# Tiles' rows in a pool of their own and loaded before the down weights, the last routing at pair 20, layernorms in other places, x of five sequences on chip

## The chip, the cores and the metric

The kernel runs on one core of one Trainium2 chip. The metric is the device time of one execution in microseconds (us); less is better. The core has five engines that work in parallel, each through its own list of instructions in order: TensorE (PE: matrix products, and transposes through an identity; its weight loads are listed apart as PEld), VectorE (DVE), ScalarE (ACT), GpSimd (POOL) and SyncE (SP). They wait for each other through semaphores. Data move between the device's memory and the on-chip SBUF by DMA; here SP issues nearly all plain loads and stores, ACT a few at the start, and POOL those whose rows are chosen by an index (scatters and gathers, "indirect"). PE writes its results to PSUM, from which DVE and ACT take them.

## The reference

Four sublayers, each with a layernorm ahead and its input added behind, on x of 8 sequences x 512 tokens x 256 features in float32:

```python
x = x + _L0_attn_ref(_layernorm(x), Wq, Wk, Wv, Wo)                  # 16 heads of 16, 4 key heads, rotary, causal
x = x + _L0_ffn_ref(_layernorm(x), router_w, w_gate, w_up, w_down)   # 32 experts of 96, each token takes 8
x = x + _L1_attn_ref(_layernorm(x), w_qkv, b_qkv, w_out, b_out)      # 16 heads of 16, causal
x = x + _L1_ffn_ref(_layernorm(x), gate_w, w1, w2, w3, sw1, sw2, sw3)# 16 experts of 176, each token takes 2, one shared of 352

def _layernorm(x, axis=-1, eps=1e-05):
    m = jnp.mean(x, axis=axis, keepdims=True)
    v = jnp.var(x, axis=axis, keepdims=True)
    return (x - m) / jnp.sqrt(v + eps)

# attention: softmax(q k^T / 4, causal) v, then the product with the out weights
# an expert layer: probs = softmax(x @ router); the k largest are a token's experts; weights rw
for e in experts:                       # layer 0: rw divided by their sum
    w_e = sum(where(sel == e, rw, 0), axis=-1)
    y += (silu(x @ wg[e]) * (x @ wu[e])) @ wd[e] * w_e[:, None]
```

## The kernel before, in words

**Stages.** The program goes through four stages: attention 0 for eight sequences (to about 609 us of the span), the experts of layer 0 (to about 1119), attention 1 (to about 1668), the experts of layer 1 (to about 1902), and a short end. `pipeline` interleaves in attention, while PE works on the scores of sequence b, the preparation of a later sequence (`before`: input, layernorm, projections) and the finish of the previous one (`finish`: `Attention.output`, then `after0` or `after1`, with layernorm, routing and in layer 1 the shared expert). The parts are Python generators; how far each is advanced at each step fixes the order of the program, and a scheduler then orders each engine's list. For PE in the expert stages the order is the written one (`manual_schedule`). `tc.issue_after(inst)` forbids that an instruction be placed ahead of `inst` in that order; it is no wait on the chip.

**Attention.** A sequence has four chunks of four heads (`NCK`). `scores` makes the products of keys and queries (L680) and their exponentials on ACT (L685), `mask` multiplies the diagonal blocks by a causal mask on DVE (L691), `values` makes the product with v (L703), copies it out (L709), transposes it (L716), and divides by the row sums on DVE: a reciprocal `rec` (L719) and a product into `otok` (L720). `output` first updates `fine` (two DVE instructions, L754 and L755), transposes `otok` (L761), multiplies by the out weights (`y_a`, L769) and adds to x.

**Layernorm.** `layernorm_steps` takes the statistics of the four tiles of 128 tokens (L315, L316), then `inverse_root` finds 1/sqrt(v) with integer arithmetic and three Newton steps (L281 to L290, a dozen small DVE instructions, each needing the one ahead of it), then xn = (x - m) * rstd (L325). `turned` transposes it on PE (L343).

**Routing.** For each sequence, `routed0` (layer 0) or `after1` (layer 1) takes the layernorm, the router's product, and the k largest (`route`). Each token's normalized row, with its weights behind it, is written to the rows of its experts in a table `xg` in device memory: 4 x 8 = 32 scatters of 128 rows per sequence in layer 0 and 4 x 2 = 8 in layer 1 (L427). Each layer's sequences fall into two parts with tables of their own: 0 to 3 and 4 to 7 in layer 0, 0 to 5 and 6 to 7 in layer 1 (`SPLIT = (4, 6)`). When a part's last sequence is routed, `tables` works out which tiles of 128 rows belong to which expert, and stores zeros behind each expert's last row (SP, L1076). In layer 0 the routing of sequence 7 isn't in attention 0 but beside the first part's experts.

**Experts.** `experts` goes through pairs of tiles of 128 rows: 75 + 75 pairs in layer 0 and 30 + 14 in layer 1. Step s of its loop does, in this order: `load` of pair s (two SP loads of 144 KB, L1141, after reading eight row numbers into registers at every fourth pair), `turn_x` of pair s - 4 (transposes L1150, copy by DVE L1152), `gate_up` of pair s - 5 (L1183, silu on ACT, products on DVE L1175), `turn_h` of pair s - 6 (L1203, copy L1204) and `down` of pair s - 7 (`y_m`, L1214, copy by ACT L1219). Layer 0 stores the result in order (SP, L1221) and gathers it by token later (POOL, L1263); layer 1 scatters it to the tokens' rows (POOL, L1225), and `results` loads them in order. At s == 3 `load_last()` issues the load of the down weights `dw` (`load_down`, L1303: six transfers in layer 0, 26 in layer 1, some 3 MB either way). PE's `y_m` for any pair reads the whole tile `dw`, whose part is chosen by a register.

The pool of `xg` tiles (seven buffers) is the pool `mp` of the other tiles of the experts, `dw` has a pool `dwp`. Pools are stacked in SBUF, and those of one stage lie where the pools of the stage before lay: the first use of an address waits for its last use there.

**Beside the experts.** `beside.add(first, last, steps, work)` spreads the steps of a generator over the pairs from `first` to `last`. In layer 0: the store of x of sequence 7, its routing (pairs 7 to 20), the tables of the second part (22 to 54), the loads of attention 1's weights, the first loads of x for attention 1 with their gathers; in layer 1: `results` of sequences 0 to 5.

**x.** `xs[b]` lives in a ring of five buffers in SBUF. After attention 0 every sequence's x is stored to `x_after[0]` and fetched again. In layer 1, `after1` stores x of sequences 0 to 5 to `x_after[1]` (`keep_x`), and `results` loads them again (`x_c`, L1331), adds the experts' results (L1348), transposes and stores the output; sequences 6 and 7 are left in their buffers.

**Start.** `fast0` loads q, k, v, cos and sin weights. k and v share the one buffer `kv_in`, cos and sin the one buffer `turnf`; those four loads are issued by ACT (L847, L858). PE turns cos and sin through transposes (L861) before the input (L1321).

Of the kernel before, what the change touches and what calls it, by code (L numbers as in the profile page):

```python
# [22 lines left out]
NG = 4  # L23
NCK = H // NG
E0, K0, I0 = 32, 8, 96
E1, K1, I1, IS1 = 16, 2, 176, 352
# [65 lines left out]
def two_blocks_kernel(  # L92
# [63 lines left out]
    def new_x(b, name):  # L156
        xs[b] = xpool.tile([P, NT, D], F32, tag="x", name=f"x_{name}_{b}", bufs=5)
        return xs[b]
# [146 lines left out]
    def layernorm_steps(x, lnp, name, tag="xn", bufs=1, spare=0, behind=lambda: None):  # L305


        def later():
            return tc.issue_after(behind()) if behind() else ExitStack()
# [12 lines left out]
        xn = lnp.tile([P, NT, D + spare], F32, tag=tag, name=f"xn_{name}", bufs=bufs)  # L322
        for t in range(NT):
            with later():
                nc.vector.tensor_scalar(  # L325
                    xn[:, t, :D], x[:, t, :], mv[:, t, 0:1], rstd[:, t : t + 1], ALU.subtract, ALU.mult
                )
            if t % 2:
                yield
        return xn  # L330
# [326 lines left out]
    class Attention:  # L657
# [6 lines left out]
        def __init__(self, n, late, ptp, ps, bank, wo, masked=None):  # L664
            self.n, self.fine, self.late, self.ptp, self.ps, self.bank, self.wo = n, fines[n], late, ptp, ps, bank, wo
            self.heads, self.otok, self.rec = {}, {}, {}
            self.last = iter(())
            self.masked = masked

# [25 lines left out]
        def values(self, b, c, probs):  # L695
# [19 lines left out]
            for t in range(NT):  # L715
# [3 lines left out]
            nc.vector.reciprocal(rec, ot[:, :, :, ONE])  # L719
            nc.vector.tensor_tensor(  # L720
                self.otok[b][:, :, c, :, :], ot[:, :, :, :DH],
                rec.unsqueeze(3).to_broadcast([P, NT, NG, DH]), ALU.mult,
            )
            yield
# [107 lines left out]
    def fast0(awp, lnp, atp, late, ptp, ps, bank):  # L832
# [11 lines left out]
        for n, which in enumerate("kv"):  # L844
            lo, hi = A0[which]
            kv_in = awp.tile([P, ND, NG, 32], F32, tag="kv_in", name=f"{which}_in", bufs=1)
            nc.scalar.dma_start(out=kv_in.rearrange("p k g r -> p (k g r)"), in_=a0[:, lo:hi])  # L847
            at = D + n * HKV * DH
            nc.vector.tensor_copy(
                wq[:, :, at : at + HKV * DH].rearrange("p k (g d) -> p k g d", g=HKV), kv_in[:, :, :, :DH]  # L850
            )
# [3 lines left out]
        for which in ("cos", "sin"):  # L855
            lo, hi = A0[which]
            f = awp.tile([DH, T], F32, tag="turnf", name=f"{which}f", bufs=1)
            nc.scalar.dma_start(out=f, in_=a0[:DH, lo:hi])  # L858
# [13 lines left out]
        def before(b):  # L872
# [4 lines left out]
            x = xs[b]  # L877
            xn = layernorm(x, lnp, name)
            yield from free()
            xn = yield from turned(xn, lnp, bank, name)  # L880
# [84 lines left out]

    def fast1(w, v1s, lnp, atp, late, ptp, ps, bank, last):
        wv, wo, vb, ob, qkb = (w[n] for n in ("v", "o", "vb", "ob", "qkb"))
        att = Attention(1, late, ptp, ps, bank, wo, last)

        def before(b):  # L970
            x, name = xs[b], f"a1_{b}"
            xn = layernorm(x, lnp, name, behind=att.masked)
            yield from free()
# [107 lines left out]
    class Beside:  # L1081


        def __init__(self, *items):
            self.items = []
            for item in items:
                self.add(*item)
            self.load = None
            self.last = None

        def add(self, first, last, steps, work):
# [13 lines left out]

    def experts(n, gu, dn, mp, ps, again, beside, load_last):

# [27 lines left out]
        def load(lay, i):  # L1135
            part = lay.part
            if i % RB == 0:
                registers(lay, i)
            xg = mp.tile([P, 2, lay.width], F32, tag="xg", name=f"xg_{name}_{part}_{i}", bufs=7)
            for j in range(2):  # L1140
# [55 lines left out]
        def turn_h(lay, i):  # L1196
# [4 lines left out]
            for q, (lo, n_in) in enumerate(chunks):  # L1201
                for j in range(2):
                    nc.tensor.transpose(hp[:n_in, q, j, :], h[:, j, lo : lo + n_in], ident)  # L1203
            beside.last = nc.vector.tensor_copy(hT[: chunks[0][1]], hp[: chunks[0][1]]).ins  # L1204
            made["hT", part, i] = hT

# [81 lines left out]

    def load_down(w, src, inner, routed):

# [7 lines left out]
        for n, lo, hi, e, at in pieces(inner, whole):  # L1298
            while lo < hi:
                q, r = at // width, at % width  # L1300
                rows = min(hi - lo, width - r)
                to = (e * chunks + q) * D
                nc.sync.dma_start(out=w[r : r + rows, :, to : to + D], in_=src[n, lo : lo + rows, :, 2 * ND * P :])  # L1303
                lo, at = lo + rows, at + rows
# [20 lines left out]
    def results(seqs, gat, op, ps, again="", behind=lambda: None):  # L1325


        def begin(b):
            if b < SPLIT[1]:
                xs[b] = gat.tile([P, NT, D], F32, tag="x", name=f"x_c1{again}_{b}", bufs=3)  # L1330
# [68 lines left out]
    def all_experts(n, gw, gat, again=False, weights=()):  # L1399
# [6 lines left out]
        with ExitStack() as s:  # L1406
            dwp = s.enter_context(tc.tile_pool(name=f"down{n}{g}", bufs=1, reuse_waits="tile"))
            mp = s.enter_context(tc.tile_pool(name=f"moe{n}{g}", bufs=3, reuse_waits="tile"))
            small = s.enter_context(tc.tile_pool(name=f"tables{n}{g}", bufs=1, reuse_waits="tile"))
            ps = s.enter_context(tc.tile_pool(name=f"ps_m{n}{g}", bufs=2, space=PSUM, reuse_waits="tile"))  # L1410
# [29 lines left out]
            if n == 0 and not again:  # L1440
                beside.add(8, 9, 1, x_kept())
                lnp = s.enter_context(tc.tile_pool(name="ln_last", bufs=1, reuse_waits="tile"))
                beside.add(7, 20, 13, routed0(NB - 1, lnp, bank, ffn_parts(lnp, bank)[0], lambda: beside.last))
                begin = 22
            beside.add(
# [48 lines left out]
    with ExitStack() as s1:  # L1494
        wp1 = s1.enter_context(tc.tile_pool(name="attn_w1", bufs=1, reuse_waits="tile"))
        gat = s1.enter_context(tc.tile_pool(name="gather", bufs=1, reuse_waits="tile"))
        w1, loads1 = weights1(wp1)
        last = all_experts(0, gw0, gat, weights=loads1)
        with ExitStack() as s:
            awp, lnp, atp, late, ptp, smp, ps = pools(s, 1, False)  # L1500
            v1s = v_tiles(awp, 2, H, nc.vector)
            bank = banks(ps, 3)
            att, before = fast1(w1, v1s, lnp, atp, late, ptp, ps, bank, last)
            route, shared = ffn_parts(smp, bank)
# [12 lines left out]
            def after1(b):  # L1517
# [58 lines left out]
    def general1(gat):  # L1576
        with ExitStack() as s:
# [20 lines left out]
            def all_of(b, name):  # L1598
# [7 lines left out]
                yield from shared(sw1, xT, xs[b], name)  # L1606
                if b < SPLIT[1]:
                    keep_x(b, x_after[1])
# [178 lines left out]
```

## Time and profile before

| | us |
|---|---|
| median of 14 runs | 1936.32 (1933.41 to 1954.11) |
| the profiled execution's own time | 1929.41 |
| its span, first to last instruction | 1927.6 |
| PE busy | 1591.6 (83%) |
| DVE busy | 993.8 (52%) |
| ACT busy | 650.0 (34%) |
| POOL busy | 811.6 (42%) |
| L427 scatters on POOL | 316.0 in 320 instructions |
| L1263 gathers on POOL | 403.6 in 256 instructions |

The mean granted clock of PE is 0.901. All engine times come from the one profiled execution, which is 0.36% shorter than the median of the runs. The chain that ended last, followed back from the end, spends 64% of the span on PE, 11% on "another core or an unknown queue", 9% on DVE, 7% on issue, 4% on ACT and 2% on DMA.

How to read it: a row of a timeline or of the chain begins with the start and the length in us, then engine and line, the operation, and the tiles written and read (`out<-in`); `x8` counts the instructions that the row takes together, and its length runs from the first one's start to the last one's end. SPq and ACTq are the queues' issues of DMAs, not the transfers. A row of waits reads: who waited, for whom, us in total, times, longest. Line numbers are those of the kernel before; in the changed kernel the same statements stand up to 20 lines lower.

### The profile page before, as it was taken

Reading aid. Unit: us, or ns where it says so; the run is one execution under the profiler, and the core shown is the slowest. Engines: PE = TensorE matmul, PEld = TensorE weight load, DVE = VectorE, ACT = ScalarE, POOL = GpSimd, SP = SyncE. Lnnn points to the kernel's source line nnn. Section 1 sums busy time; section 2 is a strip of 40 time slices with the busy share of each in tenths; the row PEclk is TensorE's granted clock in tenths of the full one; section 3 lists DMA queues with packets and bytes.
Section 4 is the critical chain, followed back from the end, with each engine's and each line's share of the span. In section 5 each row is a group of like instructions: output and inputs, shape, how many; then the busy total and the mean of one; then the engine's idle time right before and its main releaser. Section 6 shows DMA issues by size and latency. Waiting matters only on the chain.

```text
span 1927.6 us, 31020 instructions
## 1 busy us (share of the span) xinstructions
PE 1591.6 (83%) x10180; PEld 1050.0 (54%) x10180; DVE 993.8 (52%) x3179; ACT 650.0 (34%) x865; POOL 811.6 (42%) x686
## 2 busy tenths in 40 slices
PE   5976394666755758999999979998999998999995
PEld 3433142333423747989998844445444544677764
DVE  5664272544623424545555666576556645444453
ACT  3533152233312212323333335454444443222222
POOL 0041614414254160000778888488885011243332
PEclk9987696878868778999999989999999998999997
DMA  2032322522124655787999974356643022435364
GB/s 65 28 104 78 109 80 90 167 102 72 64 95 142 203 171 168 216 252 203 255 257 275 282 139 69 70 99 130 132 75 68 21 85 74 142 99 160 93 217 154
DMA packets 245721, 255.75 MB, mean 133 GB/s; under 512 B 79881, under 2 KB 224911, under 8 KB 245554
## 3 DMA queue, kind: packets, MB, share of 16 engines
q1 hardware_dynamic: 188754, 164.15, 28.6%
q0 software_dynamic: 56448, 89.18, 20.2%
q8 instruction: 88, 1.44, 0.3%
q14 instruction: 79, 0.65, 0.1%
q10 hardware_dynamic: 352, 0.33, 0.1%
HBM read 132.37 MB, written 124.32 MB: 133 GB/s over the span
## 4 chain that ended last, share of the span: by engine, by line
PE 64%; another core or an unknown queue 11%; DVE 9%; issue 7%; ACT 4%; DMA 2%; SPq 1%; POOL 0%; DVEq 0%; POOLq 0%; ACTq 0%
PE gu_m L1183 13%; PE y_m L1214 8%; PE st_a L680 8%; PE o_a L703 6%; PE xgT_m L1150 4%; ACT p_a L685 3%; PE y_a L769 3%; PE hT_m L1203 2%; PE sy_f L457 2%; PE su_f L444 2%; PE qkv_a L887 2%; PE sg_f L444 2%; DVE p_a L691 2%; PE q_a L998 2%
## 5 line engine op out<-in xcount | busy, mean ns | idle before, releaser
L427 POOL DMA_INDIRECT xg<-xn_f,rows_f x320 | 316.0, 987 | 648.3 <-DVE rec_a L719 241.2
L1263 POOL DMA_INDIRECT x_a<-yg,yrows x256 | 403.6, 1577 | 292.7 <-DVE yrows L1260 194.0
L685 ACT ACTIVATE p_a<-st_a 128x2048 f32<-128x2048 f32 (+1 forms) x192 | 306.1, 1594 | 372.9 <-PE st_a L680 229.6
L1183 PE MATMUL gu_m<-gw,xgTs_m 128*128 x1552 | 339.9, 363 | 26.7 <-DVE xgTs_m L1152 25.5
L1183 PEld LDWEIGHTS gu_m<-gw,xgTs_m 128*128 128x128 f32 x1552 | 261.6, 194 | 56.9 <-DVE xgTs_m L1152 26.9
L680 PE MATMUL st_a<-qT_a,kT_a 32*128 32x512 f32 (+3 forms) x2048 | 219.3, 502 | 60.2 <-ACT p_a L685 38.6
L1214 PE MATMUL y_m<-dw,hTs_m 96*128 (+1 forms) x952 | 239.6, 382 | 0.0
L703 PE MATMUL o_a<-p_a,v 128*32 128x512 f32 (+3 forms) x2048 | 211.3, 471 | 26.8 <-issue 20.7
L691 DVE TENSOR_TENSOR p_a<-p_a,causal 128x512 f32<-128x512 f32 x256 | 170.7, 685 | 119.7 <-ACT p_a L685 111.4
L1152 DVE COPY xgTs_m<-xgT_m 128x512 f32<-128x512 f32 x194 | 133.6, 689 | 108.5 <-PE xgT_m L1150 66.6
L680 PEld LDWEIGHTS st_a<-qT_a,kT_a 32*128 32x128 f32 x2048 | 97.7, 198 | 163.1 <-issue 77.8
L1219 ACT COPY ys_m<-y_m 128x512 f32<-128x512 f32 x194 | 113.7, 586 | 207.8 <-PE y_m L1214 150.1
L1214 PEld LDWEIGHTS y_m<-dw,hTs_m 96*128 96x128 f32 (+1 forms) x952 | 166.5, 191 | 15.5
L1175 DVE SCALAR_TENSOR_TENSOR h_m<-h_m,xg_m,gu_m 128x96 f32<-128x96 f32 (+1 forms) x388 | 114.6, 326 | 90.3 <-ACT h_m L1188 37.0
L1225 POOL DMA_INDIRECT yg<-ys_m,to_m x88 | 88.9, 1010 | 152.8 <-ACT ys_m L1219 138.2
L1204 DVE COPY hTs_m<-hT_m 96x256 f32<-96x256 f32 (+1 forms) x194 | 92.8, 478 | 116.7 <-PE hT_m L1203 77.6
L1150 PE MATMUL xgT_m<-ident,xg_m 128*128 128x128 f32 x776 | 121.9, 279 | 19.2 <-DMA xg_m<-xg 9.1
L1191 ACT ACTIVATE h_m<-gu_m 128x192 f32<-128x192 f32 x150 | 49.7, 331 | 245.7 <-PE gu_m L1183 141.5
L703 PEld LDWEIGHTS o_a<-p_a,v 128*32 128x32 f32 x2048 | 51.9, 112 | 135.8 <-issue 95.3
L709 DVE COPY osb_a<-o_a 128x512 f32<-128x512 f32 x64 | 44.0, 688 | 158.4 <-remote 61.4
L1150 PEld LDWEIGHTS xgT_m<-ident,xg_m 128*128 128x128 f32 x776 | 97.2, 144 | 43.2 <-issue 20.5
L769 PE MATMUL y_a<-wo,oT_a 128*128 128x256 f32 x256 | 78.7, 452 | 30.9 <-issue 24.1
(206 smaller groups left out, 1712.0 us busy)
## 6 DMA issues: line engine op xcount, KB each, us to landing
xg_m<-xg SPq DMA_DIRECT2D x388, 144.0 KB
yg<-ys_m SPq DMA_DIRECT2D x150, 256.0 KB
xg<-zeros SPq DMA_DIRECT2D x100, 144.0 KB
g<-yg SPq DMA_DIRECT2D x16, 512.0 KB
xg<-xn_f,rows_f POOLq DMA_INDIRECT x320
x_after<-x_in SPq DMA_DIRECT2D x8, 512.0 KB
x_a<-x_after SPq DMA_DIRECT2D x8, 512.0 KB
x_a<-yg,yrows POOLq DMA_INDIRECT x256
```

Of the source, the lines that this page charges most:

```text
L427: inst = nc.gpsimd.indirect_dma_start(out=lay.xg, out_offset=bass.IndirectOffsetOnAxis(ap=rows[:, t, i : i + 1], axis=0), in_=xn[:, t, :], ...
L680: nc.tensor.matmul(st[:, g, at : at + T - j * P], kT[r, j * P : (j + 1) * P], qT[r, j * P :], start=True, stop=True,)
L685: nc.scalar.activation(pt, st[:, :, :width], AF.Exp, scale=SCALE)
L691: self.masked = nc.vector.tensor_tensor(d, d, causal.unsqueeze(1).to_broadcast([P, NG, P]), ALU.mult).ins
L703: nc.tensor.matmul(o[32 * g : 32 * g + 32, j * P :], v1[:, j, v_at + g * (DH + 1) :][:, :32], probs[n][:, g, at : at + T - j * P], start=( ...
L769: nc.tensor.matmul(y[:, i, :], oT[:, k, t * P : (t + 1) * P], self.wo[:, k, :], start=(k == 0), stop=(k == ND - 1),)
L1150: nc.tensor.transpose(tr[:, j, c, :], xg[:, j, c * P : (c + 1) * P], ident)
L1152: nc.vector.tensor_copy(xT, tr)
L1175: nc.vector.scalar_tensor_tensor(h[:, j, :], h[:, j, :], xg[:, j, D:][:, bass.ds(offs[part, i + j][2], 1)], gus[j][:, inner:], ALU.mult, A ...
L1183: nc.tensor.matmul(gus[j], xT[:, j, c, :], gu[:, bass.ds(at + c * 2 * inner, 2 * inner)], start=(c == 0), stop=(c == ND - 1),)
L1214: nc.tensor.matmul(y[:, j, :], hT[:n_in, q, j, :], dn[:n_in, bass.ds(at + q * D, D)], start=(q == 0), stop=(q == n_ch - 1),)
L1263: nc.gpsimd.indirect_dma_start(out=xs[b][:, t, :], out_offset=None, in_=lay.yg[: lay.tiles(bool(again)) * P, :], in_offset=bass.IndirectOf ...
```

## The change

- Tiles' rows: `xg` tiles get a pool of their own, `xgp` ("rows"), opened after `mp`, with seven buffers as before. `load_down` now issues each transfer of `dw` only after the last row load that had been issued by then (`beside.load`), that is, after the eight of pairs 0 to 3.
- Last routing: the routing of sequence 7 in layer 0 goes to pairs 20 to 33 instead of 7 to 20, and the second part's tables to pairs 36 to 68 instead of 22 to 54.
- Normalizations: in attention 0, the layernorm of the next sequence may not be placed ahead of the last product into `otok` made by then, and for sequences 2 and on it is written two steps later, with as many steps fewer behind it. In attention 1, the layernorm of sequence 0 is written instruction by instruction behind the last six `hT` copies of the experts of layer 0 (two of its instructions per copy) instead of all behind the last copy.
- x: sequences 3 to 7 stay in the ring of five (`XS`); only sequences 0 to 2 are stored in `after1` and loaded in `results`.
- Start: two buffers each for `kv_in` and `turnf`.

The program that redoes the work when the fast one's bounds don't hold, which isn't run on these inputs, is changed in the same way.

```diff
+XS = 5
...
     def new_x(b, name):
-        xs[b] = xpool.tile([P, NT, D], F32, tag="x", name=f"x_{name}_{b}", bufs=5)
+        xs[b] = xpool.tile([P, NT, D], F32, tag="x", name=f"x_{name}_{b}", bufs=XS)
...
+            self.normed = None
...
-            nc.vector.tensor_tensor(
+            self.normed = nc.vector.tensor_tensor(
                 self.otok[b][:, :, c, :, :], ot[:, :, :, :DH],
                 rec.unsqueeze(3).to_broadcast([P, NT, NG, DH]), ALU.mult,
-            )
+            ).ins
...
-            kv_in = awp.tile([P, ND, NG, 32], F32, tag="kv_in", name=f"{which}_in", bufs=1)
+            kv_in = awp.tile([P, ND, NG, 32], F32, tag="kv_in", name=f"{which}_in", bufs=2)
...
-            f = awp.tile([DH, T], F32, tag="turnf", name=f"{which}f", bufs=1)
+            f = awp.tile([DH, T], F32, tag="turnf", name=f"{which}f", bufs=2)
...
             x = xs[b]
-            xn = layernorm(x, lnp, name)
-            yield from free()
+            if b > 1:
+                yield
+                yield
+            xn = layernorm(x, lnp, name, behind=att.normed)
+            for _ in range(4 if b < 2 else 2):
+                yield
             xn = yield from turned(xn, lnp, bank, name)
...
-    def fast1(w, v1s, lnp, atp, late, ptp, ps, bank, last):
+    def fast1(w, v1s, lnp, atp, late, ptp, ps, bank, copies):
-        att = Attention(1, late, ptp, ps, bank, wo, last)
+        att = Attention(1, late, ptp, ps, bank, wo, copies[-1])
...
-            xn = layernorm(x, lnp, name, behind=att.masked)
+            if b == 0:
+                behind = iter([copy for copy in copies[-6:] for _ in range(2)])
+                xn = whole(layernorm_steps(x, lnp, name, behind=lambda: next(behind)))
+            else:
+                xn = layernorm(x, lnp, name, behind=att.masked)
...
-    def experts(n, gu, dn, mp, ps, again, beside, load_last):
+    def experts(n, gu, dn, mp, xgp, ps, again, beside, load_last):
...
-            xg = mp.tile([P, 2, lay.width], F32, tag="xg", name=f"xg_{name}_{part}_{i}", bufs=7)
+            xg = xgp.tile([P, 2, lay.width], F32, tag="xg", name=f"xg_{name}_{part}_{i}")
...
             beside.last = nc.vector.tensor_copy(hT[: chunks[0][1]], hp[: chunks[0][1]]).ins
+            beside.copies.append(beside.last)
...
-    def load_down(w, src, inner, routed):
+    def load_down(w, src, inner, routed, behind):
...
-                nc.sync.dma_start(out=w[r : r + rows, :, to : to + D], in_=src[n, lo : lo + rows, :, 2 * ND * P :])
+                with tc.issue_after(behind):
+                    nc.sync.dma_start(out=w[r : r + rows, :, to : to + D], in_=src[n, lo : lo + rows, :, 2 * ND * P :])
...
         def begin(b):
-            if b < SPLIT[1]:
+            if b < NB - XS:
                 xs[b] = gat.tile([P, NT, D], F32, tag="x", name=f"x_c1{again}_{b}", bufs=3)
...
             mp = s.enter_context(tc.tile_pool(name=f"moe{n}{g}", bufs=3, reuse_waits="tile"))
+            xgp = s.enter_context(tc.tile_pool(name=f"rows{n}{g}", bufs=7, reuse_waits="tile"))
...
-                beside.add(7, 20, 13, routed0(NB - 1, lnp, bank, ffn_parts(lnp, bank)[0], lambda: beside.last))
-                begin = 22
+                beside.add(20, 33, 13, routed0(NB - 1, lnp, bank, ffn_parts(lnp, bank)[0], lambda: beside.last))
+                begin = 36
...
-            experts(n, gw, dw, mp, ps, again, beside, lambda: load_down(dw, src, inner, routed))
-            return beside.last
+            experts(n, gw, dw, mp, xgp, ps, again, beside, lambda: load_down(dw, src, inner, routed, beside.load))
+            return beside.copies
...
-                if b < SPLIT[1]:
+                if b < NB - XS:
                     keep_x(b, x_after[1])
```

More of the change, by code (lines that the diff above doesn't have):

```diff
@@ L308, in later @@
         def later():
-            return tc.issue_after(behind()) if behind() else ExitStack()
+            inst = behind()
+            return tc.issue_after(inst) if inst else ExitStack()
         stats = lnp.tile([P, NT, 6], F32, tag="stats", name=f"stats_{name}")
@@ L1089, in __init__ @@
             self.last = None
+            self.copies = []
         def add(self, first, last, steps, work):
@@ L1497, in two_blocks_kernel @@
         w1, loads1 = weights1(wp1)
-        last = all_experts(0, gw0, gat, weights=loads1)
+        copies = all_experts(0, gw0, gat, weights=loads1)
         with ExitStack() as s:
@@ L1502, in two_blocks_kernel @@
             bank = banks(ps, 3)
-            att, before = fast1(w1, v1s, lnp, atp, late, ptp, ps, bank, last)
+            att, before = fast1(w1, v1s, lnp, atp, late, ptp, ps, bank, copies)
             route, shared = ffn_parts(smp, bank)
@@ L1606, in all_of @@
                 yield from shared(sw1, xT, xs[b], name)
-                if b < SPLIT[1]:
+                if b < NB - XS:
                     keep_x(b, x_after[1])
```

## The prediction

> **What bounds the kernel now.** I read the page's engine rows first: TensorE (PE) is busy 83% of the span, so a change can only pay where PE stands still or where it would stand still afterwards. Then a table of windows cut at the stages tells where that is. Its columns are length, then busy time and instruction count of PE, weight load, VectorE (DVE), ScalarE (ACT) and GpSimd (POOL), the granted clock, the DMA share and GB/s.
>
> ```profile
> 605.00:640.00 35.00, 9.85 (x36) 7.19 (x34) 2.36 (x4) 1.87 (x2) 23.55 (x25) 0.60 0.66 203
> 640.00:655.00 15.00, 14.54 (x76) 13.81 (x77) 9.67 (x31) 3.41 (x8) 0.00 (x0) 0.80 0.83 237
> ...
> 690.00:740.00 50.00, 18.64 (x83) 15.34 (x82) 7.86 (x21) 4.47 (x10) 26.51 (x28) 0.62 0.42 141
> 740.00:820.00 80.00, 79.54 (x506) 72.93 (x505) 45.61 (x125) 24.77 (x55) 0.00 (x0) 1.00 0.69 206
> ...
> 1590.00:1670.00 80.00, 70.16 (x384) 38.95 (x383) 40.28 (x165) 21.79 (x24) 15.73 (x16) 0.89 0.36 99
> 1670.00:1766.00 96.00, 96.00 (x465) 72.50 (x465) 46.66 (x144) 22.68 (x57) 33.53 (x34) 1.00 0.42 132
> ```
>
> Two things are to be seen. Both expert stages, once running, are PE without a gap (79.54 of 80, 96.00 of 96), so a late start of either is not made up later. And in 605–640 and 690–740 every compute engine is nearly idle while POOL issues the 32 scatters of one sequence's rows (L427). By the instructions' start times there are eight such bursts of about 41 us (the first from 116.0, the last 684.5 to 725.3), and in each the gaps over 1 us that PE, DVE and ACT have together sum to 13.5 to 26.3 us. I call that the standstill; its cause is not in the profile, and the bursts of 8 scatters in attention 1 show none.
>
> Then the waits of PE at the places the diff touches, the start of the chain that ended last, and SyncE (SP), which issues the loads:
>
> ```profile
> PE oT_a L761 <- DVE rstd_a L290: 1.8, 1, 1.8
> PE o_a L703 <- DVE p_a L691: 0.4, 1, 0.4
> ...
> PE xT_a L343 <- DVE xn_a L325: 3.3, 1, 3.3
> ```
> ```profile
> 1.25 2.42 DMA cosf<-in_a_dram
> ...
> 4.42 4.98 DMA sinf<-in_a_dram
> ```
> ```profile
> 600.99 2.57 SPq L1303 DMA_DIRECT2D dw<-in_f_dram  x4
> 604.63 34.32 SPq L1141 DMA_DIRECT2D xg_m<-xg  x8
> 638.96 1.40 SPq L1303 DMA_DIRECT2D dw<-in_f_dram  x2
> ...
> 1624.61 13.86 SPq L1303 DMA_DIRECT2D dw<-in_f_dram  x26
> 1639.60 9.27 SPq L1141 DMA_DIRECT2D xg_m<-xg  x14
> ```
> ```profile
> 646.74 1.03 PE L1214 MATMUL y_m<-dw,hTs_m 96*128 x4
> ...
> 1678.76 1.89 PE L1214 MATMUL y_m<-dw,hTs_m 88*128 x8
> 1680.48 0.60 PE L1150 MATMUL xgT_m<-ident,xg_m 128*128 128x128 f32 x4
> ```
>
> **The change, part by part,** against the profiled execution: 1929.41 us, span 1927.6 (1.8 around it), 6.9 us or 0.36% under the median 1936.32 of 14 runs. I take each difference over to the median unchanged.
>
> *Start of attention 0 (two buffers for kv_in and turnf).* The load of sinf is issued at 4.42, after cosf's buffer is free, and lands 4.98 later. PE takes its transposes first (9.45) and the input's behind them (9.99), though xf had landed by 6. With two buffers sinf and v_in are issued some 2.5 us earlier. Next in line on DVE is q_in's copy (landed 8.45, 0.62 us) and the bias (9.21), and the changed order puts stats_a ahead of five small instructions. I put stats_a's first instruction at 9.9 instead of 11.76, where the chain shows it: −2, between −0.5 (q_in is late too) and −3.5.
>
> *Layernorm behind the last normalization in attention 0.* At the one clean turn from a sequence to the next (75 to 90), stats and the 14-step rstd chain stand on DVE ahead of the reciprocal and product that oT needs: PE waits 1.8 + 0.4 us. The same DVE work now comes behind; its xn is needed only 60 us later, so it costs nothing there: −2.2. Six more turns lie in or at the edge of a burst, where the waits shown (8.8, 11.6 and 23.1 us) contain the standstill. Each is worth between 0, if the standstill covers it, and 2.2; I take 1: −6 (0 to −13).
>
> *Layernorm of attention 1's first sequence, woven behind the last hT copies.* The row of 3.3 us goes: 5.7 us of DVE work starts behind the last six pairs instead of after the last. A pair lasts 2.83 us and DVE is busy 45.61 of 80 in it, so some 1.2 us per pair are free: over five pairs it fits. It may delay hT copies by one 0.4 us instruction each. −3, between −4 and −1.
>
> *Rows ahead of down weights, experts 0.* Now the first xg load waits for the last y_a of attention (ends 608.8), and six dw loads (3.15 MB) go behind eight xg loads. Before, four of them (2.05 MB) went at 601 to 603.6 and landed during the standstill, at no cost. In it, SP gets on at 0.70 us per item, 4.2 us for a pair of loads; the second pair, which also waited for y_a, got through at 619.4 (SP's own rows), which I take for the first now, three more pairs reach 632 to 636, and dw is issued by about 639. At the 237 GB/s of the row for 640–655, 3.15 MB take 13.3 us: landed at 652 to 653 against a first y_m at 646.74. Nothing else of PE can pass y_m. +6, between +2 (the loads get through early) and +12 (the next pair's rows, queued behind dw, come after it).
>
> The Trainium skill (DMA: Bandwidth & Descriptors, "Anatomy of one DMA") fits a transfer, measured on GpSimd's path, at 2.0 us plus its bytes over 436 GB/s. By it dw would be there 9.2 us after its issue, an estimate from that page, at 648, and this term would be +1.5. The window row shows 237 GB/s with the engines 83% taken, so I stay with the row.
>
> *The same, experts 1.* Before, the 26 dw loads were out by 1638.5, 40 us ahead of the first y_m. Now the first xg load waits for the shared expert's su of sequence 6 (about 1642, harmless) and the second pair for all eight scatters of sequence 7, whose issues end at 1664.9; I take 1666.5 for their landing, about as long after as an issue and a half. Three pairs need 2.6 us, the 26 loads 13.9 as before, about 2 us to land the last (cosf's 32 KB took 2.42): some 1685 against 1678.76. The fifth pair's rows, behind dw, land near 1687 against 1680.48. Both give +6 to +7, and the second is covered by the first. +6, between +2 (2.88 MB at 237 GB/s need only 12.2 us from 1668.5) and +12 (scatters land later).
>
> *Last routing at pairs 20 to 33 instead of 7 to 20.* Its PE and DVE instructions and POOL's 32 scatters are the same; POOL has no other DMA between 725 and the gathers from 919, so its order stays. The burst meets the same kind of pairs, and what it stops is again PE-bound. The tables go from pairs 22–54 to 36–68, and with them 33 stores of zeros (144 KB each) on SP's queue, still ahead of the second part's first load at pair 75; the yg stores there go past single xg loads. 0, between −13 (a standstill of 13.5, the least seen, for 26.3) and +10 (the zeros meet the prefetch).
>
> *x of five sequences on chip.* Three stores of 512 KB in attention 1 and three loads in experts 1 (issued 1858, 1869, 1880) go, and results of sequences 3 to 5 take a step less each. DMA share there is 0.36 to 0.48, SP is not on the chain, and the end hangs on the last scatter, its load and two additions, all unchanged: 0, between −2 and 0.
>
> Sum: −2 − 2.2 − 6 − 3 + 6 + 6 = −1.2. Span 1926.4, execution 1928.2, median about **1935 us**.
>
> **The rivals.** 0.3% (5.8 us) is about what a measurement of this kernel can tell from no change: under 1930.5 is faster, over 1942.1 slower.
>
> Slower: dw behind the rows, at both stages. For it: PE cannot go round y_m, and the rates are the trace's. If the six turns in bursts give 0, the start −0.5, attention 1 −1, and both waits are +12: −2.2 − 1.5 + 24 = +20, 1956. It decides once the waits together exceed what the layernorms give by 6. Against it: SP may leave the standstill sooner.
>
> Faster: all seven turns give 2.2 (−15.4), start −3.5, attention 1 −4, both waits +2: −19, 1917. For it: the rows of waits are there at each turn, and DVE holds 9% of the chain. Against it: a standstill takes whatever lies in it.
>
> The standstill changes with its place: 13.5 instead of 26.3 takes 13 off, 1922; a collision adds 10, 1945. For it: the spread of the eight; against: the two bursts beside expert work were the long ones.
>
> That keeping x on chip changes nothing is in the sum already.
>
> **How the numbers follow.** The sum (own range 1928 to 1942) 0.35: 0.08 of that faster, 0.25 same, 0.02 slower. Late weights 0.31: 0.29 slower, 0.02 same. All turns paying 0.25, faster. Another standstill 0.09: 0.06 faster, 0.03 slower. So 0.39, 0.27, 0.34. The range 1916 to 1957 reaches both outer cases.
>
> **What would show it.** Stats of sequence 0 near 9.9; no wait of oT for rstd at 80; xT right behind the last y_m of experts 0; first y_m waiting for dw's DMA, 6 us later against the last y_a and against the end of attention 1; the standstill of the last burst near 26 us. The prediction fails if the bursts in attention 0 change length, since their sum of 170 us is far above every term here, or if dw gets out before the standstill ends.

## The result

| | us |
|---|---|
| before, median (47 runs) | 1936.57 (1931.63 to 1958.35) |
| changed, median (10 runs) | 1961.51 (1957.42 to 1974.45) |
| ratio, 95% interval | 1.0124 [1.0095, 1.0153] |
| changed, the profiled execution | 1947.03, span 1945.3 |

The changed kernel is 1.2% slower; the median lies 4.5 us above the predicted range. The two profiled executions differ by 17.6 us, the medians by 25: the profiled execution is 14.5 us under the median of the changed kernel, where that of before was 6.9 under its own.

The experiments further down ran on four chips on which all times are some 14% lower: the kernel before has a median of 1658 to 1660 us on each of them, and the changed kernel is 1.0019 [1.0003, 1.0036] of it. How the two settings differ is told with the experiments; first the two traces of the first setting, which the prediction was about.

The start of the same instruction in both traces shows where the time went (us of the span; the last column is what the stretch since the row above gained or lost):

| place | before | changed | difference | of it in this stretch |
|---|---|---|---|---|
| first stats of attention 0 | 11.76 | 9.59 | -2.2 | -2.2 |
| last y_a of sequence 0 (end) | 92.07 | 85.64 | -6.4 | -4.3 |
| last y_a of sequence 4 (end) | 416.46 | 406.21 | -10.3 | -3.8 |
| last y_a of sequence 7 (end) | 608.81 | 605.40 | -3.4 | +6.8 |
| first y_m of layer 0 | 646.74 | 648.80 | +2.1 | +5.5 |
| pair 15 | 682.07 | 682.94 | +0.9 | -1.2 |
| pair 35 (past both routings) | 777.62 | 780.54 | +2.9 | +2.1 |
| pair 75 | 896.78 | 904.44 | +7.7 | +4.7 |
| first xT_a of attention 1 | 1121.93 | 1126.64 | +4.7 | -3.0 |
| last y_a of attention 1 (end) | 1632.30 | 1638.41 | +6.1 | +1.4 |
| first y_m of layer 1 | 1678.76 | 1693.87 | +15.1 | +9.0 |
| pair 8 of layer 1 | 1700.97 | 1719.53 | +18.6 | +3.4 |
| end of PE | 1918.35 | 1937.10 | +18.8 | +0.2 |

The windows of the changed kernel, the same as of before and four more around the start of layer 1 (columns as there):

```profile
605.00:640.00 35.00, 9.93 (x33) 6.98 (x33) 3.79 (x9) 1.83 (x3) 21.23 (x23) 0.65 0.62 181
640.00:655.00 15.00, 9.74 (x40) 8.77 (x40) 3.69 (x10) 1.36 (x4) 0.00 (x0) 0.68 0.98 236
...
690.00:740.00 50.00, 44.78 (x288) 41.12 (x286) 28.12 (x107) 15.66 (x31) 10.90 (x12) 0.97 0.65 198
740.00:820.00 80.00, 54.52 (x312) 48.47 (x313) 29.59 (x86) 16.30 (x36) 19.88 (x21) 0.81 0.53 161
...
1670.00:1766.00 96.00, 89.04 (x405) 65.97 (x404) 42.62 (x133) 18.37 (x46) 26.35 (x28) 0.93 0.52 148
...
1674.00:1684.00 10.00, 6.83 (x22) 4.31 (x23) 3.86 (x19) 0.63 (x2) 0.00 (x0) 0.66 0.85 214
1684.00:1694.00 10.00, 6.45 (x32) 4.39 (x31) 4.42 (x10) 1.27 (x4) 0.00 (x0) 1.00 0.89 199
1694.00:1702.00 8.00, 8.00 (x22) 5.56 (x23) 2.80 (x14) 0.91 (x2) 2.00 (x2) 0.57 0.88 262
1702.00:1720.00 18.00, 18.00 (x94) 13.94 (x92) 8.41 (x24) 4.25 (x11) 5.91 (x6) 1.00 0.44 147
```

In 640 to 655 PE is busy 9.74 of 15 us where it had been 14.54, and the DMA engines are full (0.98, 236 GB/s): the down weights are on their way. In layer 1 the 96 us that had been without a gap hold 7 us of idle time, and in two short stretches the granted clock is 0.66 and 0.57 where it had been 1.00. Cut at the clock's own changes, these are two stretches of 6.8 us at half the clock, with full clock between them:

```profile
1677.13:1683.95 6.82, 5.41 (x11) 3.31 (x12) 2.42 (x9) 0.63 (x2) 0.00 (x0) 0.50 0.84 197
1683.95:1694.19 10.24, 6.69 (x33) 4.61 (x32) 4.55 (x10) 1.27 (x5) 0.00 (x0) 1.00 0.89 202
1694.19:1701.02 6.83, 6.83 (x18) 4.80 (x17) 2.41 (x13) 0.91 (x2) 2.00 (x2) 0.50 0.86 256
```

The standstill has moved from 690–740 to 740–820.

PE's and SP's timelines of the changed kernel at the two starts:

```profile
633.87 3.51 SPq L1319 DMA_DIRECT2D dw<-in_f_dram  x6
637.58 12.66 SPq L1155 DMA_DIRECT2D xg_m<-xg  x9
...
1648.85 26.20 SPq L1155 DMA_DIRECT2D xg_m<-xg  x8
1675.16 14.04 SPq L1319 DMA_DIRECT2D dw<-in_f_dram  x26
1690.32 7.25 SPq L1155 DMA_DIRECT2D xg_m<-xg  x12
```
```profile
648.80 2.04 PE L1229 MATMUL y_m<-dw,hTs_m 96*128 x4 [5.26 <-DMA xg_m<-xg]
...
1678.54 5.06 PE L1197 MATMUL gu_m<-gw,xgTs_m 128*128 x8 [2.69 <-DVE xgTs_m L1166]
...
1684.11 2.53 PE L1197 MATMUL gu_m<-gw,xgTs_m 128*128 x8
...
1693.87 3.44 PE L1229 MATMUL y_m<-dw,hTs_m 88*128 x8 [3.55 <-DMA xg_m<-xg]
1697.10 1.06 PE L1164 MATMUL xgT_m<-ident,xg_m 128*128 128x128 f32 x4
1697.95 4.05 PE L1197 MATMUL gu_m<-gw,xgTs_m 128*128 x8
```

The brackets put y_m's waits down to a row load, but it is dw that came late: among the semaphores that y_m waits for is that of the last dw load, and the trace has its last update at 648.71 in layer 0 and at 1693.73 in layer 1, where y_m begins at 648.80 and 1693.87. In layer 1 that load was issued at 1688.85, so it took 4.9 us to land.

Added up by PE's time, the 12.4 us of layer 1 (9.0 to the first y_m, 3.4 more to pair 8) have three parts. PE stands 2.69 us since DVE's list has small `to_m` instructions of later pairs ahead of the first copy of xT, and four of those wait for rows that come late (2.1 us together); it stands 3.55 for dw. The third part is the slower clock: the same eight gu_m matmuls take 5.06 and 4.05 us where they take 2.53 at full clock, and y_m 3.44 for 1.89; that is 5.6 us, nearly as much as both stops together. Along the path these parts don't all count. y_m begins when dw is there, whatever PE did before, so the first stop and the slow gu_m after it lie inside the wait for dw. The 9.0 us are the late dw, and the 3.4 behind them are the half clock after the second stop.

And the zeros of the second part's tables (SP's timeline, and PE's waits from 820 to 905), which now lie in pairs 55 to 68:

```profile
840.67 4.48 SPq L1089 DMA_DIRECT2D xg<-zeros  x9
...
863.28 3.99 SPq L1089 DMA_DIRECT2D xg<-zeros  x8
...
874.76 5.06 SPq L1089 DMA_DIRECT2D xg<-zeros  x8
```
```profile
PE xgT_m L1164 <- DMA xg_m<-xg: 5.1, 3, 2.2
PE xgT_m L1164 <- DMA yg<-ys_m: 0.8, 1, 0.8
```

A batch of eight or nine stores holds SP's queue for 4 to 5 us, and PE waits for late rows three times. In the kernel before, the batches lay among the same loads of attention 1's weights (from pair 37 on in both kernels) and PE waited less (waits from 780 to 900):

```profile
793.71 4.47 SPq L1076 DMA_DIRECT2D xg<-zeros  x9
...
806.98 4.35 SPq L1076 DMA_DIRECT2D xg<-zeros  x8
```
```profile
PE xgT_m L1150 <- DMA xg_m<-xg: 3.2, 4, 2.5
```

### The profile page after: what moved, and what is told of

It is laid out like the page before. It is cut to its first block, busy times and chain, and to the rows that moved or that the text cites. A ratio compares the mean times of both kernels' runs of the same rounds, so it can differ in the third digit from the quotient of the medians.

```text
span 1945.3 us, 31005 instructions
## 1 busy us (share of the span) xinstructions
PE 1594.6 (82%) x10180; PEld 1054.0 (54%) x10180; DVE 993.1 (51%) x3179; ACT 649.8 (33%) x865; POOL 809.5 (42%) x686
## 5 line engine op out<-in xcount | busy, mean ns | idle before, releaser
L1197 PE MATMUL gu_m<-gw,xgTs_m 128*128 x1552 | 346.3, 368 | 27.9 <-issue 19.1
L1197 PEld LDWEIGHTS gu_m<-gw,xgTs_m 128*128 128x128 f32 x1552 | 265.8, 197 | 60.2 <-issue 23.8
L706 PE MATMUL o_a<-p_a,v 128*32 128x512 f32 (+3 forms) x2048 | 206.6, 469 | 11.1 <-issue 5.9
L1217 PE MATMUL hT_m<-ident,h_m 128*96 128x128 f32 (+1 forms) x476 | 85.1, 276 | 23.0 <-DVE h_m L1189 18.8
```

Of the source, the lines that this page charges most:

```text
L706: nc.tensor.matmul(o[32 * g : 32 * g + 32, j * P :], v1[:, j, v_at + g * (DH + 1) :][:, :32], probs[n][:, g, at : at + T - j * P], start=( ...
L1197: nc.tensor.matmul(gus[j], xT[:, j, c, :], gu[:, bass.ds(at + c * 2 * inner, 2 * inner)], start=(c == 0), stop=(c == ND - 1),)
```

## The experiments

On the experiments' chips no standstill is seen in the bursts of attention 0 ahead of its last sequence: in e4's trace 128 scatters run from 115 to 298 us with at most 4.5 us between two, and from 115 to 400 us PE, DVE and ACT share no idle time in gaps over 1 us. The chain and the time of attention 0 change with it (400 us instead of 609). So these runs price the parts of the change without standstills. Differences of place are taken against the trace of e4, which is within 0.1% of the kernel before. A run's profiled execution lies up to 5 us from its median (e4's 4.3 above, e5's 4.9 above, e1's 4.4 below), so the traces tell where time goes, and the medians how much.

**e4: x of five sequences on chip, alone.** Before plus:

```diff
-        xs[b] = xpool.tile([P, NT, D], F32, tag="x", name=f"x_{name}_{b}", bufs=5)
+        xs[b] = xpool.tile([P, NT, D], F32, tag="x", name=f"x_{name}_{b}", bufs=XS)
...
-            if b < SPLIT[1]:
+            if b < NB - XS:
```

> The kernel before with only x of five sequences kept on chip. Theory (three stores and three loads that nothing waited for): within 3 us, ratio 0.9985 to 1.0015. Rival (the end of attention 1, which is 3.8 us later in the changed kernel in sequences 6 and 7, is later because of it): the last y_a of attention 1 comes 3 to 4 us later, ratio 1.002.

Measured: 1.0007 [0.9990, 1.0023]. It changes nothing; the late end of attention 1 isn't its doing as far as this can tell.

**e5: the changed kernel itself.**

> The changed kernel as it is, beside the parts of it. If this chip shows standstills in the scatter bursts: ratio 1.010 to 1.015 as first measured. If it shows none (the kernel before at some 1658 us): theory (late weights cost 14 us there, half of them made good by less crowded rows at pair 10) ratio 1.000 to 1.005; rival (the loss was the standstills' alone) ratio 0.990 to 0.994, like the layernorms' kernel.

Measured: 1.0019 [1.0003, 1.0036], the theory's range. Its first y_m in layer 0 waits still longer here, 14.3 us:

```profile
PE y_m L1229 <- DMA xg_m<-xg: 14.3, 1, 14.3
```

Against e4's trace it is only 1.1 us behind at the first y_m, since attention 0 ends 10 us earlier, and 10.9 us ahead at pair 10, since e4's kernel stops some 11 us between pairs 8 and 10. There the routing of sequence 7 has DVE wait for the scatters of the sequence before, and PE waits behind DVE:

```profile
438.81 0.74 DVE L326 TENSOR_SCALAR xn_f<-x_in,mv_f,rstd_f 128x256 f32<-128x256 f32 x2 [9.61 <-DMA xg<-xn_f,rows_f]
```
```profile
PE gu_m L1184 <- DVE xgTs_m L1153: 7.8, 1, 7.8
```

Both the routing's later place and the late start avoid this stop: pairs 8 and 9 take 17.5 us in e4, 5.7 in the changed kernel, 5.7 in e1 and e11 (told of below; early, routing at pair 20) and 6.6 in e2 (late, routing at pair 7).

**e1: the down weights ahead again.** The changed kernel with

```diff
-            experts(n, gw, dw, mp, xgp, ps, again, beside, lambda: load_down(dw, src, inner, routed, beside.load))
+            experts(n, gw, dw, mp, xgp, ps, again, beside, lambda: load_down(dw, src, inner, routed, None))
```

(with None, nothing holds the loads back.)

> The changed kernel with one part undone: the down weights' loads are no longer held back behind the row loads, the rows keep their own pool. Theory (late down weights): both expert stages lose their late start, 5 to 6 us before the first y_m of layer 0 and some 9 of the 12 us in layer 1 (its stalls for dw and the lower granted clock after them go; the wait for the rows themselves, about 3, stays): 14 us less than the changed kernel, 1.0124 falls to about 1.005. Rival (the rows' own pool is what is late, since its first loads wait for attention's last reads): the first y_m stays where it is in both stages and the time changes by under 4 us.

Measured: 0.9929 [0.9911, 0.9948], against 1.0019 for the changed kernel: 9.0 thousandths or 15 us, as the theory had it in size; the rival of under 4 us falls. The places differ from the theory: against e5's trace e1 is 10.4 us ahead at the first y_m of layer 0 and 14.2 at pair 75, and layer 1 adds 6.8 from the end of attention 1 to its pair 8, where the theory had 5 to 6 and 9. PE at the start of layer 1, and the first row of the same place in the kernel before:

```profile
1378.44 0.66 PE L1164 MATMUL xgT_m<-ident,xg_m 128*128 128x128 f32 x4 [0.72 <-DVE out_of L1397]
...
1383.01 4.15 PE L1197 MATMUL gu_m<-gw,xgTs_m 128*128 x8 [3.20 <-DVE xgTs_m L1166]
...
1393.48 1.89 PE L1229 MATMUL y_m<-dw,hTs_m 88*128 x8
```
```profile
1668.36 0.66 PE L1150 MATMUL xgT_m<-ident,xg_m 128*128 128x128 f32 x4 [0.72 <-DVE out_of L1381]
```

The wait of y_m and its slow clock are gone, while the wait behind the late rows stays: 15.0 us from the first transposes to the first y_m, where the kernel before takes 10.4 (y_m at 1678.76). These 4.6 us are the price of the rows' own pool at this place when the weights are early; in the changed kernel they lie inside the wait for dw.

**e2: the last routing at pair 7 again.** The changed kernel with

```diff
-                beside.add(20, 33, 13, routed0(NB - 1, lnp, bank, ffn_parts(lnp, bank)[0], lambda: beside.last))
-                begin = 36
+                beside.add(7, 20, 13, routed0(NB - 1, lnp, bank, ffn_parts(lnp, bank)[0], lambda: beside.last))
+                begin = 22
```

> The changed kernel with one part undone: last routing at pairs 7 to 20 and tables at 22 to 54 again. Theory (the move costs through the zeros' stores, which meet the loads of attention 1's weights and rows in pairs 55 to 68, and not through the standstill): pair 75 comes 4 to 7 us earlier against the first y_m of layer 0, the ratio falls from 1.0124 to 1.009 or 1.010. Rival (the place of the burst costs nothing): within 2 us, 1.0124 stays.

Measured: 0.9988 [0.9974, 1.0001], 3.1 thousandths or 5 us under the changed kernel. Pairs 15 to 75 cost 1.2 us more than in e4's kernel here and 10.1 more in the changed one, so the trace has nearly 9 us for the move where the medians have 5. It shows where the zeros are: pairs 60 to 75 take 53.9 us in the changed kernel and 42.4 in e2's and e4's.

**e3 and e6: the start and both layernorms, alone.** The kernel before with the changed kernel's lines for `kv_in`, `turnf`, `normed` and `copies`, and nothing else; run twice, on two chips.

> The kernel before with only the two buffers at the start and both layernorms moved. Theory (the turns in attention 0 gain about 2 us each, seven of them, and the start and attention 1 gain 2 and 3): 15 to 20 us faster, ratio 0.990 to 0.992. Rival (what the turns gain is taken or given by the length of the standstills, which depends on how the lists of instructions lie against the bursts): attention 0 ends only 3 to 5 us earlier, as in the changed kernel, ratio 0.996 to 0.999.

> The kernel before with the two buffers at the start and both layernorms moved, once more. With standstills: theory (their length is what decides) ratio 0.994 to 1.000, although seven turns are shorter; rival (the turns pay in full everywhere) 0.990. Without standstills: 0.989 as before.

Measured: 0.9890 [0.9873, 0.9906] and 0.9890 [0.9862, 0.9918]: 18 to 19 us faster. In the first of them attention 0 ends 12.3 us earlier, and 4 more come at the first xT_a of attention 1. What comes between is a shorter stop at pairs 8 to 10.

**e9: the turns alone.** The kernel before with only

```diff
+            if b > 1:
+                yield
+                yield
-            xn = layernorm(x, lnp, name)
-            yield from free()
+            xn = layernorm(x, lnp, name, behind=att.normed)
+            for _ in range(4 if b < 2 else 2):
+                yield
```

> The kernel before with only the layernorm of attention 0 moved, without the two buffers at the start and without the layernorm of attention 1. Without standstills: theory (nearly all of the layernorms' kernel's gain in attention 0 is the turns) 10 to 12 us earlier at the last y_a of attention 0, ratio 0.992 to 0.994. With standstills: theory (their lengths decide) between 4 us earlier and 4 later at that place, ratio 0.996 to 1.003; rival (the turns pay in full everywhere) 10 us earlier, ratio 0.994.

Measured: 0.9951 [0.9934, 0.9968]. Attention 0 ends 8.9 us earlier, somewhat under what was expected: the first four turns give 3.2, 3.8, 2.6 and 3.5 us, and between sequences 4 and 7 some 4.4 are lost again. So a turn is worth more than the 2.2 that the wait before showed, but not at every sequence.

**e11, e12, e7: the place and the spreading.** On top of e3's kernel, e11 has the last routing at pair 20, e12 stores the zeros two by two, e7 has both:

```diff
-                for rows in at:
-                    inst = nc.sync.dma_start(out=lay.xg[rows, :], in_=zeros[:, : lay.width])
-                    ...
-            yield
+            for few in range(0, len(at), 2) if beside else [0]:
+                for rows in at[few : few + 2] if beside else at:
+                    with tc.issue_after(beside.load) if beside else ExitStack():
+                        inst = nc.sync.dma_start(out=lay.xg[rows, :], in_=zeros[:, : lay.width])
+                    ...
+                yield
...
-                begin, min(32 + begin, first - 4), 6 + lays[n][1].n_e // 8, tables(
+                begin, min(32 + begin, first - 4), 7 + lays[n][1].n_e // 2, tables(
```

> The layernorms' kernel with the last routing at pairs 20 to 33 and tables at 36 to 68, the zeros' stores eight at a time as in the changed kernel. Theory (the place pays at pairs 8 to 15, the bunched zeros among the weights' loads take it back at pairs 55 to 70): no better than the layernorms' kernel, ratio 0.988 to 0.992, with 8 to 12 us lost between pairs 60 and 75. Rival (the spreading did nothing, the place alone made the better kernel): ratio 0.986.

> The layernorms' kernel with the zeros' stores two by two, the routing left at pairs 7 to 20. Theory (spread zeros save what the bunches cost at pairs 50 to 60, some 3 to 4 us, and the place is worth the rest): ratio 0.986 to 0.989, between the layernorms' kernel and the one with both. Rival (spreading alone makes the better kernel): ratio 0.986 or under.

> The layernorms' kernel with the last routing at pairs 20 to 33 too, tables at 36 to 68, their 33 stores of zeros spread two by two over the pairs instead of eight at a time. Theory (the routing's new place pays some 9 us at pairs 8 to 15, and what it lost was the crowding of the zeros' stores): without standstills 5 to 9 us under the layernorms' kernel, ratio 0.984 to 0.986. Rival (the zeros' bytes cost what they cost, in any order): no difference to the layernorms' kernel, within 2 us.

(Line numbers shift by a few between these kernels.) Measured: e3's kernel 0.9890; place alone 0.9860 [0.9838, 0.9883]; spread alone 0.9883 [0.9860, 0.9906]; both 0.9859 [0.9835, 0.9884]. In the traces, PE's waits from 560 to 630 us in e11:

```profile
PE xgT_m L1161 <- DMA xg_m<-xg: 5.7, 3, 2.4
PE xgT_m L1161 <- DMA yg<-ys_m: 0.9, 1, 0.9
```

and in e7:

```profile
PE xgT_m L1163 <- PE y_m L1228: 0.6, 1, 0.6
PE xgT_m L1163 <- DMA xg_m<-xg: 0.2, 1, 0.2
```

Against e6's trace (e7's is of the same chip, e11's of another), e11 is 9.2 us ahead at pair 60 and 0.5 behind at pair 75, as the theory had it (its time isn't: 0.9860 is what the rival had); e7 is 11.3 ahead and 10.1 ahead. So the spread stores do take these waits away in the profiled execution. The times don't follow: place alone and both are the same, and all four intervals overlap. By the medians the place gains 3 thousandths on a kernel whose weights and rows aren't late (the stop at pairs 8 to 10 is where its trace gains), which the intervals leave uncertain; in the changed kernel, whose late start skips that stop, the same place costs 5 us. That spreading makes the kernel faster isn't shown. e7 is the fastest by its median, 1635 us against 1658 of the kernel before and 1662 of the changed one.

**e8 and e10: scatters in groups.** On top of e3's kernel, the `rows` of each tile of 128 tokens are computed later, one tile every six steps of the attention, and its eight scatters with them:

```diff
+                if held and n % 6 == 2:
+                    held.pop(0)(att.masked)
```

> The layernorms' kernel with each sequence's 32 scatters in attention 0 let go in four groups of eight, one every six steps of the attention, instead of all at once. Theory (the engines stand still since their lists of instructions are not fetched while a long burst runs): on a chip with standstills they nearly vanish in attention 0 (from some 145 us to under 40), 80 us or more faster; without standstills no more than 5 us of difference. Rival (each scatter costs the engines its share, in a burst or alone): the idle time stays, and the time too.

> The layernorms' kernel with the scatters of attention 0 in four groups of eight, once more, for a chip with standstills. There: theory (long bursts keep the lists of instructions from being fetched) idle time of all engines in attention 0 from some 145 us to under 40, 80 us or more faster than the kernel before; rival (each scatter costs its share) idle time and ratio like the layernorms' kernel. Without standstills it repeats 0.991.

Measured: 0.9907 [0.9882, 0.9931] and 0.9919 [0.9896, 0.9943], 2 to 3 thousandths over e3's kernel. For the standstills this decides nothing: none of the chips showed them, and POOL, with 41 us of scatters for some 43 to 46 us of attention a sequence, ran the groups back to back all the same (128 from 111 to 284 us in e8). Whether groups would end the standstills where they occur is open.

## Why the prediction was wrong

**Right.** The start (-2 forecast, -2.2 at the first statistics). The rows ahead of the weights in layer 0 (+6, and +5.5 from the last y_a to the first y_m), with some luck: dw was issued 28.5 us after the last y_a where the forecast had 30.2, and took 1.5 us longer. There a page was weighed against a row: dw was issued from 633.87 on, by the row of 237 GB/s it is there 13.3 us after its first issue, at 647.2, by the fit of the Trainium skill (DMA: Bandwidth & Descriptors, "Anatomy of one DMA") 9.2 after, at 643, an estimate from that page; the trace has its last landing at 648.71, 14.8 us after, and the window shows 236 GB/s with the engines full. The row was the nearer. The layernorm of attention 1 (-3, and -3.0 from pair 75 to its first xT_a, and -4 in e3). x on chip (0, and 1.0007). That the standstill of the moved burst would be the same (26.3 and 25.8 us).

**Wrong, in the first setting.** The sum was -1.2 where the profiled executions differ by +17.6. Three terms make nearly all of it.

1. *Experts 1: +6 with a bound of +12; measured +12.4.* Up to the last issue of dw the step was right: counted from the end of attention 1, the first dw load went out where it was forecast (6.1 us later in the span, as attention 1 ended 6.1 later), and the 26 issues took 14.0 us (forecast 13.9). Two things failed. "About 2 us to land the last", taken from cosf's 32 KB, was 4.9, and that is nearly all of what makes 9.0 of 6.2 at the first y_m. And the step ended at y_m's start: it put nothing for the half clock after the stop, which cost 3.4 us more by pair 8. It also left out what the late rows of pairs 1 to 3 stop on DVE (2.69 us of PE's time, the clock behind it 2.5), but here dw's wait covered that; e1, with dw early, has it alone (4.6).
2. *Last routing: 0, measured +6.8 from pair 15 to pair 75.* The step said of the zeros only that they are ahead of the part's first load, and put nothing for them: of the 6.8 us, 4.7 are lost from pair 35 to 75, where PE waits 5.1 us for rows. The upper bound, +10 ("the zeros meet the prefetch"), held it. e2 gives 5 us for the whole move. Why the zeros cost more there than at pairs 40 to 54, where they lay among the same weights' loads, isn't shown.
3. *Turns: -8, measured -8.1 by sequence 4, then +6.8 to sequence 7.* Without standstills they are worth -8.9 (e9). The loss stands in one stretch, 7.9 us from sequence 4 to 5. The burst in it had 19.9 us of standstill after 16.3 before, which is 3.6 of it; but 2.9 us are lost in the same stretch in e3, e5 and e9, where nothing stands still, so the standstill is only a part, and what makes the other isn't shown. (The next burst stood 15.3 us after 13.5, in a stretch that gained 0.6.) The prediction named a change of the bursts' length as what would make it fail, yet the width of its six turns, 0 to -13, left no room for a loss.

**Wrong in the way the sum was carried over.** The last 7.6 us of the miss aren't in the profiled executions at all: taking the difference over to the median "unchanged" assumed that a profiled execution stands to its median as before. It stood 6.9 us under it before and 14.5 now; with one such execution of each kernel, why isn't known.

**What is open.** In the experiments' setting the layernorms and the start (0.9890), x on chip (+0.0007), the late weights as measured with the routing at pair 20 (+0.0090) and the routing's place as measured with late weights (+0.0031) give 1.0018, and 1.0019 was measured. That looks as if nothing were left for the own pool, but the place alone, without late weights, is -0.0030 (e11). Going one by one from e3 over x and e11's place, e1 (0.9929) lies 0.0062 higher, some 10 us, and what it has beyond them is the own pool; its own trace shows 4.6 us of that at one place. So place and late weights aren't independent, and the own pool has a price, whose size the runs give only roughly. In the first setting the same change costs 1.0 points more; as no run of the parts fell into that setting, what each part costs there isn't shown. Of the rivals, the slower one (late weights, 1956) had the larger part of the mechanism; it was put at 0.31. That its +20 lies near the +17.6 measured is partly luck: its +12 in layer 0 was 5.5, and the routing's 6.8 wasn't in it.

## What to carry to other kernels

A load that is held back behind others has to be costed to the landing of its last part, with the queue as full as it will be then (here 4.9 us, not the 2.4 of a small load at the start), and each stop of TensorE with the slower clock after it: here 3.4 us behind a stop of 3.55. When two parts of a change act on the same stop, measure each with and without the other before adding them up. When a step is moved, look at what its stores and loads meet on the queue at the new place. And before adding small gains in a stage, look whether something larger there varies from one version to the next: a sum of 2 us terms says little beside 170 us of standstills.

## What the runs showed of the hardware

The standstills have a trace of their own. The DMA queues of the kernel before in the middle of one of its bursts (from 285 to 315 us; packets, MB, share of 16 engines):

```profile
q0 software_dynamic: 1142, 3.54, 32.1%
q1 hardware_dynamic: 144, 0.52, 6.5%
```

and of e4's kernel, where nothing stands still, from 200 to 230 us, nearly all within two bursts that follow each other:

```profile
q0 software_dynamic: 966, 2.96, 26.5%
q1 hardware_dynamic: 925, 0.67, 9.4%
q8 instruction: 2, 0.03, 0.4%
q14 instruction: 1, 0.01, 0.1%
```

With about as many scatter packets, the queues that bring instructions moved nothing in the first. By the packets' own times, the kernel before has no instruction packet between 279.64 and 329.79, between 592.43 and 645.84 and between 679.66 and 731.45, and none for 25 to 48 us in each of the other five bursts; ahead of them and between them one comes every 21 us or oftener. The engines stop some 10 to 17 us into a burst and go on within some 5 us of its end. The Trainium skill (Runtime: NRT & Kernel Launch, "Instruction fetch mechanics") has each engine fetch its next page of 16 KiB through a DMA queue while it executes the current one, and calls the cost mostly hidden; the packets of 16 KB on one of the two instruction queues agree (those of the other have 8 KB). That the engines stood still for want of instructions fits all of this, and then the cost wasn't hidden in these bursts. But it was argued from the packets and not tested, and a gap alone doesn't make a standstill: between 1110.13 and 1141.39 no instruction packet comes either, and no gap over 1 us is shared by the engines there. Why the four chips of the experiments fetch through the same bursts (in e4, 128 scatters with at most 4.5 us between two) isn't known.

The granted clock answers to short stops. In the changed kernel, two stops of TensorE at the start of layer 1, 2.69 and 3.55 us long, each brought 6.8 us at 0.50, which began within 1.5 us of the stop's end; after that it was at 1.00 again. In e5's trace the same two stops, 2.58 and 3.87 us, brought 3.4 and 6.8 us at 0.50, and in e1's one of 3.20 brought 3.4.
